# A graph layer's edge pipeline: gathers wait for a nearer sum, two quads go last, additions one step later

## The chip, the cores and the metric

The kernel runs on one core of a Trainium2 chip. TensorE (PE) multiplies matrices, VectorE (DVE) and ScalarE (ACT) work element by element, GpSimd (POOL) issues the indirect DMAs of this kernel, and SyncE (SP) issues most of the other DMAs. The metric is the device time of one execution in microseconds, lower being better.

## The reference, cut to what matters

```python
HIDDEN, NUM_RBF, CUTOFF = 128, 50, 10.0
src, dst = (edge_index[0], edge_index[1])
rbf = jnp.exp(-(distances[:, None] - centers) ** 2 / (2.0 * width * width))
cut = 0.5 * (jnp.cos(jnp.pi * distances / CUTOFF) + 1.0) * (distances <= CUTOFF)
W = (silu(rbf @ fw1 + fb1) @ fw2 + fb2) * cut[:, None]
messages = (h[src] @ pw + pb) * W
agg = jax.ops.segment_sum(messages, dst, num_segments=num_atoms)
L0 = h + (silu(agg @ mw1 + mb1) @ mw2 + mb2)
out = layernorm(x + L0)
```

The call's inputs set the sizes: x has 12,500 rows of 128, and there are 400,000 edges, sorted by destination, with lengths drawn up to 12 and then scaled by 4.688. An edge longer than 10 gives nothing, since its cut is zero. Everything is float32.

## The kernel before

The edges that are no longer than 10 are packed first, in seven chunks, and worked in 139 *quads* (`NL`) of 4 x 128 edges. One step of the main loop does one quad q, and pieces of its neighbours:

- `fetches` issues the indirect DMAs (`fetch`, L1074) that bring the rows `proj[src]` of the quads ahead, four to a quad (`j` 0 to 3), on POOL's queue. The first twelve quads gather x itself and are multiplied by `pw` later (`multiplies`). Eight quads (`SINGLY`) get their j = 0 rows by single-row copies on SP (L1064) and have three gathers. How far ahead POOL runs is set while the program is written: by an estimated clock, by the buffers, and by a wait that `fetch` puts on a gather, for the sum that stood last but `FOLLOW` in the list `last_sum` then.
- `radials` loads the lengths of two quads (tile d) on SP, `basis` makes the radial functions on ACT (L1121, L1122), `first` is the filter's first layer on PE (L1130), `silu` its activation on ACT (L1136); each works on two quads at a time. `second` is the second layer on PE (L1144, L1147), two steps ahead of the quad's message.
- `message` multiplies filter and gathered rows on DVE (L1158). `place` writes the one-hot matrices on DVE (tile hot, L1170) that send each edge to its node within a window of nodes and carry the cutoff factor. `sum_up` multiplies both on PE (L1190), and `add` adds the window to aggT on DVE (L1223).
- `nodes` and `tail` do the node layers as groups of up to four 128-node tiles become complete: `node_first` (L1233, L1234, ACT L1238), `node_second` (L344, L347), the residual and statistics (`node_stats`, L1254, L1259), `deviations` (L1266 to L1270), `scales` (L1277, L1278) and `normalize` (DVE or POOL L1289, ACT L1292), then a store (`node_dma`, L178).

Packing a chunk runs beside the steps: DVE works out where each near edge goes, a scatter on POOL's queue writes the lists (L507, once a chunk), SP loads them back (tile pair), and DVE unpacks them (L852, L853, L882) with transposes on PE (L917). The lists are cleared beforehand by `clear_packed` on SP.

The engines' queues hold what the program's text gives them, in that order; there is no other planner. The order of quads is plain, but for one: `quad_of` takes out the quad `LAST`, which is summed as the very last step, in quarters (`last` in `last_step`), since it belongs to the node tile `END` = 3 alone. Everything after that quad has to end with it: add, node layers, layer norm and store of tile 3.

Of the kernel before, what the change touches and what calls it, by code (L numbers as in the profile page):

```python
# [20 lines left out]
P = 128  # L21
# [8 lines left out]
FOLLOW = 3  # L30
QE = QT * P
# [13 lines left out]
LAST = 26  # L45
# [12 lines left out]
OWN_4 = 66  # L58
DIRECT = 32
# [12 lines left out]
SINGLY = (22, 44, 62, 67, 86, 102, 118, 133)  # L72
# [7 lines left out]
READY = {80: 9, 84: 6, 88: 5, 90: 4}  # L80
# [6 lines left out]
def kernel(  # L87
# [61 lines left out]
    def load_x(t0, n=None):  # L149
        t = x4_sb[loaded[0] % X_BUFS]  # L150
        loaded[0] += 1
        node_dma(t0, t, x, False, n)
        x_sb[t0] = t
# [26 lines left out]
    def quad_of(q):  # L180

        return q if q < LAST or q >= NL else LAST if q == NL - 1 else q + 1

    def steps(k):

        return k if k <= LAST or k >= NL else k - 1
# [637 lines left out]
    def unpack(c):  # L824
# [132 lines left out]
        if QB[c] <= LAST < QB[c + 1]:  # L957
            k = 2 * (LAST - QB[c])
            upto, that = (work.tile([64, 1], F32, name=n, bufs=1)[:np_] for n in ("upto", "that"))
            nc.vector.scalar_tensor_tensor(that, ident[:np_, k:k + 1], -1.0, ident[:np_, k + 1:k + 2],  # L960
                                           op0=OP.mult, op1=OP.subtract)
# [106 lines left out]
    def fetch(q, idx=None, table=None, js=range(QT)):  # L1068
        got = quad_sb[place_of(q) if q >= 0 else 0]
        for j in js:  # L1070
# [6 lines left out]
            if table is None and idx is None and len(last_sum) > FOLLOW:  # L1077
                tc.add_manual_dep(ins.ins, last_sum[-1 - FOLLOW], mybir.DependencyInfo(
# [9 lines left out]
    def radial(o, lengths, eng=nc.sync):  # L1088

        n = math.prod(lengths.shape) // QE  # L1090
        d = work.tile([P, QE], F32, name="d", bufs=3)
        v = lengths.rearrange("(o h) e -> o h e", o=1)
        eng.dma_start(d, v.to_broadcast([64, 2, QE]))
        d_of[o] = d, n
# [3 lines left out]
    def radials(to):  # L1098

        while next_o[0] < min(to, -(-NL // 2)):  # L1100
# [3 lines left out]
            a, b = 2 * quad_of(quads(o)[0]), 2 * quad_of(quads(o)[-1]) + 2  # L1104
            assert b - a == 2 * len(quads(o))
            radial(o, near_d[a:b].rearrange("(h t) e -> h (t e)", t=2))
# [99 lines left out]
    def bases_of(q0, q1):  # L1206

        _, v = nc.values_load_multi_w_load_instructions(
# [3 lines left out]
        for k in range(2 * (q1 - q0)):  # L1212
            bases[q0 + k // 2, k % 2] = v[k]
# [525 lines left out]
```

## Time and profile before

| what | value |
|---|---|
| median of 3 runs | 719.06 us (718.80 to 720.36) |
| profiled execution | 719.15 us |
| its span, first to last instruction | 717.5 us |
| mean granted TensorE clock | 0.917 |
| busy: PE / DVE / ACT / POOL | 590.3 / 561.8 / 397.3 / 536.4 us |
| HBM read / written | 74.59 / 15.79 MB |

The busy times are shares of one span, and no engine reaches it: PE is busy 82%, DVE 78%, POOL 75%, ACT 55%. For POOL the figure leaves out the time between two DMA issues of its own, which the profile books as idle and "issue". In a row of groups stand the line, the engine, the operation, its output and inputs, the count, the busy time with the mean of one in ns, and the idle time before it with what ended most of it. In a timeline row stand the start, the duration, the operation, and in brackets the idle time before it. A row of windows gives the stretch, its length, the busy time of PE, PEld, DVE, ACT and POOL with their instruction counts, the granted PE clock, the DMA engines' busy share and GB/s.

### The profile page before, as it was taken

How to read it: one execution, taken by the hardware profiler on the slowest of the kernel's cores; microseconds unless marked ns; L12 is line 12 of the kernel's file. 1: busy time of each engine (PE TensorE's matmuls, PEld its weight loads, DVE VectorE, ACT ScalarE, POOL GpSimd, SP SyncE). 2: the span in 40 equal slices, each digit the busy share in tenths (PEclk: the TensorE clock that was granted, in tenths of full speed). 3: DMA queues.
4: the chain of work that ended last, by engine and by line, in shares of the span. 5: the costliest groups of instructions: out<-in, count | busy, mean ns of one | idle time of the engine just before them, and what ended most of it. 6: DMA issues, size and time to landing. Idle time of an engine off the chain costs nothing. (4 is left out here: it accounts for less than half of the span.)

```text
span 717.5 us, 13667 instructions
## 1 busy us (share of the span) xinstructions
PE 590.3 (82%) x3524; PEld 465.0 (65%) x3524; DVE 561.8 (78%) x1736; ACT 397.3 (55%) x564; POOL 536.4 (75%) x576
## 2 busy tenths in 40 slices
PE   6887877898889889888588896999987878878884
PEld 5775556776667667576466674787765655656663
DVE  8899799787988999899689895878655455565685
ACT  6557624563645566464348253858744833574474
POOL 7777777777777777777777777777777777777773
PEclk9999687997988999999979997999998999999998
DMA  8995442343334334343333343444433433244342
GB/s 263 348 324 174 149 128 75 87 137 100 98 86 121 97 95 108 97 128 83 94 106 113 98 119 103 137 127 135 136 97 99 148 92 114 84 141 134 96 130 91
DMA packets 53389, 91.35 MB, mean 127 GB/s; under 512 B 13856, under 2 KB 21120, under 8 KB 53306
## 3 DMA queue, kind: packets, MB, share of 16 engines
q1 hardware_dynamic: 34754, 53.20, 22.9%
q0 software_dynamic: 17840, 36.77, 19.8%
q8 instruction: 29, 0.48, 0.3%
q10 hardware_dynamic: 712, 0.46, 0.2%
q14 instruction: 54, 0.44, 0.2%
HBM read 74.59 MB, written 15.79 MB: 126 GB/s over the span
## 5 line engine op out<-in xcount | busy, mean ns | idle before, releaser
L1074 POOL DMA_INDIRECT quad<-proj,srci x421 | 400.6, 952 | 128.4 <-issue 97.6
L1147 PEld LDWEIGHTS bank<-fw_sb,s 128*128 128x128 f32 x1112 | 160.8, 208 | 66.5 <-issue 59.8
L1136 ACT ACTIVATE s<-ph 128x1024 f32<-128x1024 f32 x70 | 71.3, 1018 | 184.4 <-PE ph L1130 184.3
L1147 PE MATMUL bank<-fw_sb,s 128*128 128x128 f32 x1112 | 161.8, 293 | 0.0
L1130 PE MATMUL ph<-rbf,w_sb 102*128 102x512 f32 x278 | 147.1, 655 | 7.5 <-ACT rbf L1122 3.9
L1190 PEld LDWEIGHTS sums<-hot,msg 128*128 128x128 f32 x816 | 112.0, 204 | 54.9 <-issue 27.4
L1170 DVE TENSOR_SCALAR hot<-iota_n,dl,cut 128x80 f32<-128x80 f32 (+4 forms) x408 | 110.1, 344 | 23.6 <-PE sums L1190 21.7
L1190 PE MATMUL sums<-hot,msg 128*128 128x80 f32 (+4 forms) x816 | 113.7, 285 | 15.4 <-DVE msg L1156 7.7
L1144 PE MATMUL bank<-fb_b,ones_b 96*128 96x512 bf16 x139 | 56.1, 404 | 48.8 <-DVE msg L1158 29.8
L1074 POOL DMA_INDIRECT x<-proj,srci x79 | 75.0, 949 | 24.1 <-issue 19.8
L1158 DVE TENSOR_TENSOR msg<-bank,quad 128x512 f32<-128x512 f32 (+1 forms) x82 | 55.7, 679 | 39.4 <-DMA quad<-proj,srci 36.9
L1130 PEld LDWEIGHTS ph<-rbf,w_sb 102*128 102x128 f32 x278 | 52.8, 211 | 48.1 <-issue 38.8
L1223 DVE TENSOR_TENSOR aggT<-aggT,sums 128x80 f32 (+4 forms) x209 | 54.0, 258 | 32.5 <-PE bank L1234 11.7
L1121 ACT ACTIVATE rbf<-d,rbf_bias,rbf_scale 102x512 f32<-102x512 f32 x70 | 56.2, 803 | 14.8 <-DMA d<-near_d 14.7
L1074 POOL DMA_INDIRECT quad<-in_x_dram,srci x48 | 47.6, 992 | 14.8 <-issue 11.9
L347 PEld LDWEIGHTS bank<-pw_sb,xT 128*128 128x128 f32 (+1 forms) x292 | 42.0, 207 | 8.0 <-issue 4.0
L1122 ACT ACT_TABLE_LOAD x35 | 44.9, 1283 | 0.6
L1136 ACT ACT_TABLE_LOAD x35 | 44.9, 1283 | 0.6
L1122 ACT ACTIVATE rbf<-rbf 102x512 f32<-102x512 f32 x70 | 44.1, 630 | 1.5
L1190 PE MATMUL sums<-quad,quad 128*128 128x104 f32 (+3 forms) x296 | 40.9, 281 | 3.9 <-DVE quad L1158 3.9
L1170 DVE TENSOR_SCALAR quad<-iota_n,dl,cut 128x104 f32<-128x104 f32 (+3 forms) x148 | 40.5, 348 | 3.9 <-issue 2.8
L1158 DVE TENSOR_TENSOR quad<-bank,quad 128x512 f32<-128x512 f32 (+2 forms) x40 | 25.2, 632 | 23.4 <-DMA quad<-proj,srci 16.1
(282 smaller groups left out, 803.0 us busy)
## 6 DMA issues: line engine op xcount, KB each, us to landing
d<-near_d SPq DMA_DIRECT2D x70, 256.0 KB
dl<-proj SPq DMA_DIRECT2D x1024, 0.5 KB
x<-in_x_dram SPq DMA_DIRECT2D x45, 256.0 KB
quad<-proj,srci POOLq DMA_INDIRECT x421
proj<-hp SPq DMA_DIRECT2D x24, 256.0 KB
out_dram<-x SPq DMA_DIRECT2D x21, 256.0 KB
r_d<-in_edge_weight_dram SPq DMA_DIRECT2D x5, 256.0 KB
r_dst<-in_dst_dram SPq DMA_DIRECT2D x5, 256.0 KB
```

Source lines behind the costliest of these rows:

```text
L347: nc.tensor.matmul(to[:m, k, :], lT[:, k * P:k * P + m], w, start=False, stop=(k == a + c - 1))
L1074: ins = nc.gpsimd.indirect_dma_start(out=got[:, j, :], out_offset=None, in_=proj if table is None else table, in_offset=bass.IndirectOffse ...
L1121: nc.scalar.activation(rbf[:u], d[:u], AF.Square, bias=rbf_bias[:u], scale=rbf_scale[:u])
L1122: nc.scalar.activation(rbf[:u], rbf[:u], AF.Exp, scale=-1.0 / (2.0 * width * width))
L1130: nc.tensor.matmul(ph[:, h, :], w1_sb[:2 * KR, h, :], rbf[:2 * KR], start=True, stop=True)
L1136: nc.scalar.activation(s[:, :n], ph[:, :n], AF.Silu)
L1144: nc.tensor.matmul(pu, ones_b[:, :P], bias_b["fb2"].rearrange("k j f -> k (j f)"), start=True, stop=False)
L1147: nc.tensor.matmul(pu[:, j * H:(j + 1) * H], s[:, j * P:(j + 1) * P], fw2_sb, start=False, stop=(j == QT - 1))
L1158: nc.vector.tensor_mul(msg[:, a:b, :], pu_of[q].rearrange("p (j f) -> p j f", j=QT)[:, a:b, :], got_of[q][:, a:b, :])
L1170: nc.vector.tensor_scalar(hot[:, j, :wide(q)], iota_n[:, :wide(q)], dl[:, at[0], at[1]], cut[:, at[0], at[1]], op0=OP.is_equal, op1=OP.mult)
L1190: ins = nc.tensor.matmul(pa[:, k * W:k * W + wide(q)], msg[:, j, :], hot[:, j, :wide(q)], start=(j % n == 0), stop=(j % n == n - 1))
L1223: nc.vector.tensor_add(to, to, pa[:, k * W:k * W + wide(q)])
```

## The change

Five things are changed.

1. A gather that is written once twenty sums stand in the program (`NEARER`) waits for the sum one further back than the newest (`NEAR` = 1), where it was three further back.
2. The additions of a step come after the next step's message on DVE, up to 15 steps from the end.
3. `first` and `silu` are issued in every even step, once, where it was in steps 0 and 1 of every four; from step 32 on (`SHIFT`) they run one pair of quads further ahead, and `basis` moves with them.
4. Two quads, 25 and 26, are left for the last two steps, where it was 26 alone. The other node groups move a step earlier (`READY`, `tail`), and `last_step` is written anew: tile 3 has its residual added on PE by a product with the identity, its statistics by bn_stats and bn_aggr, and one scaling. Its rows are loaded at step 70 and doubled on ACT at step 74.
5. The clears of `packed` are four DMAs in place of fourteen, d is loaded in two pieces where its quads aren't neighbours, and the SINGLY quads 44 and 67 become 43 and 66.

The diff, cut to its core:

```diff
+NEARER = 20
+NEAR = 1
...
-LAST = 26
+LAST = 25
+N_LAST = 2
...
+SHIFT = 32
...
-SINGLY = (22, 44, 62, 67, 86, 102, 118, 133)
+SINGLY = (22, 43, 62, 66, 86, 102, 118, 133)
...
-READY = {80: 9, 84: 6, 88: 5, 90: 4}
+READY = {80: 9, 84: 7, 88: 6, 90: 5, 93: 4, 95: 3}
...
+        late = q - (NL - N_LAST)
+        return q if q < LAST or q >= NL else LAST + late if late >= 0 else q + N_LAST
...
-            if table is None and idx is None and len(last_sum) > FOLLOW:
-                tc.add_manual_dep(ins.ins, last_sum[-1 - FOLLOW], mybir.DependencyInfo(
+            back = FOLLOW if len(last_sum) < NEARER else NEAR
+            if table is None and idx is None and len(last_sum) > back:
+                tc.add_manual_dep(ins.ins, last_sum[-1 - back], mybir.DependencyInfo(
...
-        for i in range(LISTS if k == 0 else 3):
-            v = packed[i, a:b].rearrange("(p w) -> p w", p=P)
-            for w0 in range(0, (b - a) // P, 376):
-                n = min(376, (b - a) // P - w0)
-                eng.dma_start(v[:, w0:w0 + n], zero_i[:, :n])
+        m = LISTS if k == 0 else 3
+        v = packed[:m, a:b].rearrange("s (p w) -> p s w", p=P)
+        for w0 in range(0, (b - a) // P, 376):
+            n = min(376, (b - a) // P - w0)
+            eng.dma_start(v[:, :, w0:w0 + n], zero_i[:, None, :n].to_broadcast([P, m, n]))
...
-    def last_step(q, msg):
+    def last_step(q):
         assert not ready and not deep and not singles
-        bases_of(q, NL - 1)
-        roots = deviations([84, 88, 90], st_of[3][:, 4:])
-        nc.scalar.activation(warm, half_pi, AF.Silu)
+        place(q)
+        node_stats(93, st_of[1][:, 9:])
+        msg = message(q)
+        node_second(95)
         tc.mark_branch_hint_location("rest", some, [
             mybir.EngineType.DVE, mybir.EngineType.PE, mybir.EngineType.Pool])
-        keep_busy(5)
+        keep_busy(2)
         sum_up(q, msg)
-        assert done_to(2 * q + 2) >= 95 * P
-        node_first(93)
+        node_stats(95, st_of[1][:, 11:])
+        nc.scalar.activation(warm, half_pi, AF.Sqrt)
         def last(j):
             sum_up(NL - 1, message(NL - 1, (j, j + 1)), (j,))
         last(0)
+        roots = deviations([84, 88, 90, 93, 95], st_of[1])
+        nc.scalar.activation(warm, half_pi, AF.Silu)
+        add(q)
+        keep_busy(2)
+        last(1)
         scales(*roots)
-        add(q)
-        node_first(95)
-        last(1)
-        normalize(*ready.pop(0))
-        for n in (2, 3):
-            normalize(*ready.pop(0), on=range(n), v=nc.gpsimd)
-        node_second(93)
+        of = {r[0]: r for r in ready}
+        ready.clear()
+        normalize(*of[93], on=range(2))
+        normalize(*of[90])
+        normalize(*of[84], on=range(4), v=nc.gpsimd)
+        keep_busy(2)
         last(2)
-        node_second(95)
+        keep_busy(1)
+        pz, py = bank(), bank()
+        nc.tensor.matmul(pz[:, :P], bias_b["mb1"][:, 0, :], ones_b[:, :P], start=True, stop=False)
+        nc.tensor.matmul(py[:, :H], ones_b[:, :P], bias_b["mb2"][:, 0, :], start=True, stop=False)
+        nc.tensor.matmul(py[:, :H], ident, end_sb[:, 0, :], start=False, stop=False)
         last(3)
-        node_stats(93, st_of[1], lambda: add(NL - 1))
-        node_first(END)
-        node_stats(95, st_of[1][:, 2:])
-        node_second(END)
-        node_stats(END, st_of[1][:, 5:])
-        scales(*deviations([93, 95, END], st_of[1]))
-        normalize(*ready.pop(0), on=(0, 1), v=nc.gpsimd)
-        normalize(*ready.pop(0), on=(0, 1), eng=nc.scalar)
-        normalize(*ready.pop(0), on=(0,))
-        assert not ready
+        add(NL - 1)
+        normalize(*of[95], on=range(3))
+        normalize(*of[88], on=range(2), v=nc.gpsimd)
+        nc.tensor.matmul(pz[:, :P], mw1_sb, aggT[:, END * P:(END + 1) * P], start=False, stop=True)
+        zs = work.tile([P, QE], F32, name="zs", tag="hp", bufs=3)[:, :P]
+        nc.scalar.activation(zs, pz[:, :P], AF.Silu)
+        nc.tensor.matmul(py[:, :H], zs, mw2_sb, start=False, stop=True)
+        st, mv = keep.tile([P, 6], F32, name="st_end"), keep.tile([P, 2], F32, name="mv_end")
+        nc.vector.bn_stats(st, py[:, :H])
+        nc.vector.bn_aggr(mv, st)
+        dev = keep.tile([P, 2], F32, name="dev_end")
+        nc.scalar.activation(dev[:, 0:1], mv[:, 1:2], AF.Sqrt, bias=eps)
+        nc.vector.reciprocal(dev[:, 1:2], dev[:, 0:1])
+        nc.vector.tensor_scalar(end_sb[:, 0, :], py[:, :H], mv[:, 0:1], dev[:, 1:2],
+                                op0=OP.subtract, op1=OP.mult)
+        free.extend((pz, py))
+        node_dma(END, end_sb, out, True)
...
         msg = message(q)
+        while to_add:
+            add(to_add.pop(0))
...
+        if q == NODES:
+            node_dma(END, end_sb, x, False)
+        if q == NODES + 4:
+            nc.scalar.activation(end_sb, end_sb, AF.Copy, scale=2.0)
         if loads_later and q >= 8:
             nc.sync.dma_start(*loads_later.pop(0))
-        radials(q // 2 + 5)
+        radials(q // 2 + (5 if q < SHIFT else 6 + q % 4 // 2))
         one_by_one()
         multiplies(q + 1 + EARLY_X)
         if q + 2 < NL:
             second(q + 2)
-        if q % 4 < 2 and 2 * octs(q) < NL:
-            first(octs(q))
-            silu(octs(q))
-        if q % 4 == 3:
+        while q % 2 == 0 and 2 * ahead[0] < min(NL, q + (6 if q < SHIFT else 8)):
+            first(ahead[0])
+            silu(ahead[0])
+            ahead[0] += 1
+        if q % 4 == (3 if q < SHIFT else 1):
...
-            add(k)
+            if q < NL - 15:
+                to_add.append(k)
+            else:
+                add(k)
         tail(q)
```

How the rows of the engines' queues move, at three places. The lines of the kernel after are some ten higher: L1141 for L1130, L1155 and L1158 for L1144 and L1147, L1169 for L1158, L1181 for L1170, L1201 for L1190 and L1225 for L1223.

PE at steps 16 to 18, before (ph is the first layer's output, bank the second layer's, sums the window sums):

```order
260 L1130 MATMUL ph<-rbf,w_sb 128x512 x2
261 L1190 MATMUL sums<-hot_1071,msg_1076 128x56 x4
262 L1144 LDWEIGHTS ones_b
263 L1144 MATMUL bank_168<-fb_b,ones_b 128x512
264 L1147 MATMUL bank_168<-fw_sb,s 128x128 x4
265 L1130 MATMUL ph<-rbf,w_sb 128x512 x2
266 L1190 MATMUL sums<-hot_1190,msg_1218 128x56 x4
267 L1144 LDWEIGHTS ones_b
268 L1144 MATMUL bank_170<-fb_b,ones_b 128x512
269 L1147 MATMUL bank_170<-fw_sb,s 128x128 x4
270 L1190 MATMUL sums<-hot_1071,msg_1076 128x56 x4
```

and after:

```order
260 L1141 MATMUL ph<-rbf,w_sb 128x512 x2
261 L1201 MATMUL sums<-hot_1065,msg_1070 128x56 x4
262 L1155 LDWEIGHTS ones_b
263 L1155 MATMUL bank_168<-fb_b,ones_b 128x512
264 L1158 MATMUL bank_168<-fw_sb,s 128x128 x4
265 L1201 MATMUL sums<-hot_1184,msg_1208 128x56 x4
266 L1155 LDWEIGHTS ones_b
267 L1155 MATMUL bank_170<-fb_b,ones_b 128x512
268 L1158 MATMUL bank_170<-fw_sb,s 128x128 x4
269 L1141 MATMUL ph<-rbf,w_sb 128x512 x2
270 L1201 MATMUL sums<-hot_1065,msg_1070 128x56 x4
```

The first layer that stood ahead of the sum of step 17 now stands ahead of that of step 18; step 17 has none.

DVE at steps 15 and 16, before (msg is the message, hot the one-hot matrices, the ISA rows set an addition's address, nodes and r_d belong to packing):

```order
391 L1158 TENSOR_TENSOR msg_1218<-bank_170,x_90 128x512
392 L1200 TENSOR_LOAD base_i x2
393 L1170 TENSOR_SCALAR hot_1071<-iota_n,dl,cut 128x56 x4
394 L1223 ISA
395 L1223 TENSOR_TENSOR aggT<-aggT,sums 128x56
396 L1223 ISA
397 L1223 TENSOR_TENSOR aggT<-aggT,sums 128x56
398 L532 SCALAR_TENSOR_TENSOR nodes<-bank_167,nodes 128x512
399 L522 COPY_PREDICATED nodes<-bank_167,nodes 128x448
400 L522 COPY_PREDICATED r_d<-bank_167,r_d 128x448
401 L1158 TENSOR_TENSOR msg_1076<-bank_169,x_91 128x512
```

and after:

```order
392 L1169 TENSOR_TENSOR msg_1208<-bank_170,x_90 128x512
393 L1211 TENSOR_LOAD base_i x2
394 L1181 TENSOR_SCALAR hot_1065<-iota_n,dl,cut 128x56 x4
395 L537 SCALAR_TENSOR_TENSOR nodes<-bank_167,nodes 128x512
396 L527 COPY_PREDICATED nodes<-bank_167,nodes 128x448
397 L527 COPY_PREDICATED r_d<-bank_167,r_d 128x448
398 L1169 TENSOR_TENSOR msg_1070<-bank_169,x_91 128x512
399 L1225 ISA
400 L1225 TENSOR_TENSOR aggT<-aggT,sums 128x56
401 L1225 ISA
402 L1225 TENSOR_TENSOR aggT<-aggT,sums 128x56
403 L1181 TENSOR_SCALAR hot_1184<-iota_n,dl,cut 128x56 x4
```

The two additions left the place behind the one-hot matrices of step 15 and stand behind the message of step 16.

DVE at the very end, before (end is tile 3, x_90 the group at tile 95, st the statistics):

```order
1573 L1259 BN_STATS st<-x_90 128x6 x2
1574 L1259 BN_STATS st<-x_90 84x6
1575 L1254 SCALAR_TENSOR_TENSOR end<-end,bank_170 128x128
1576 L1259 BN_STATS st<-end 128x6
1577 L1266 TENSOR_TENSOR dif<-st 128x6
1578 L1267 TENSOR_TENSOR both_m<-st 128x12
1579 L1268 SCALAR_TENSOR_TENSOR dif<-dif 128x6
1580 L1269 TENSOR_TENSOR v<-both_m,dif 128x6
1581 L1277 RECIPROCAL rs<-dev 128x6
1582 L1278 SCALAR_TENSOR_TENSOR by<-both_m,rs 128x6
1583 L1289 TENSOR_SCALAR x_90<-x_90,rs,by 128x128 x2
1584 L1289 TENSOR_SCALAR end<-end,rs,by 128x128
```

and after:

```order
1547 L1169 TENSOR_TENSOR quad_79<-bank_168,quad_86 128x128 x2
1548 L1225 ISA
1549 L1225 TENSOR_TENSOR aggT<-aggT,sums 128x80
1550 L1291 TENSOR_SCALAR x_90<-x_90,rs,by 128x128 x2
1551 L1291 TENSOR_SCALAR x_90<-x_90,rs,by 84x128
1552 L1428 BN_STATS st_end<-bank_170 128x6
1553 L1429 BN_AGGR mv_end<-st_end 128x2
1554 L1432 RECIPROCAL dev_end<-dev_end 128x1
1555 L1433 TENSOR_SCALAR end<-bank_170,mv_end,dev_end 128x128
```

Group 95 is scaled ahead of the last tile's statistics, the addition of the residual and five small operations are gone, and the scaling reads PSUM.

More of the change, by code (lines that the diff above doesn't have):

```diff
@@ L1204, in base_of @@
             bases[q, k] = v[0]
[L1206 to L1213 removed]
     def added(q):
[L1217 removed]
+        return max((q - 2) // 2 * 2 if q < NL - 14 else q - 1 if q < NL - 5 else q, 0)
     def add(q, ks=(0, 1)):
@@ L1559 @@
     clock[0] += 1.3
-    def octs(q):
-        return q // 4 * 2 + 2 + q % 4
-    some, counted = None, []
+    some, counted, to_add, ahead = None, [], [], [2]
     for q in range(NL - 2):
```

66 lines of the change are left out of this document (34 added, 32 removed).

## The prediction, made before the changed kernel ran

> **What bounds the kernel now.** I read the page's costliest groups first, then the waits of POOL and DVE, the busy time by windows, and the timelines of the places where the change can act. The first row says where the time goes: 421 of the indirect gathers, which POOL issues itself.
>
> ```profile
> L1074 POOL DMA_INDIRECT quad<-proj,srci x421 | 400.6, 952 | 128.4 <-issue 97.6
> L1074 POOL DMA_INDIRECT x<-proj,srci x79 | 75.0, 949 | 24.1 <-issue 19.8
> L1074 POOL DMA_INDIRECT quad<-in_x_dram,srci x48 | 47.6, 992 | 14.8 <-issue 11.9
> ```
>
> Each row has the busy time, the mean length in ns, and the idle time ahead. 421 + 79 + 48 = 548 gathers, and their busy and idle time sum to 400.6 + 75.0 + 47.6 + 128.4 + 24.1 + 14.8 = 690.5 us of the 717.5 us span. POOL's longest list of waits is this:
>
> ```profile
> POOL quad L1074 <- issue: 109.5, 359, 0.3
> ```
>
> The third number is the longest wait: no gather counted there waited more than 0.3 us. So POOL waits for nobody; it spends its own 1.26 us for each gather (690.5 / 548), from the first to the last. The windows show the same belt in the middle and near the end (PE, PEld, DVE, ACT, POOL busy us in 20 us, each with its instructions):
>
> ```profile
> 440.00:460.00 20.00, 19.32 (x110) 14.41 (x110) 13.53 (x53) 13.30 (x21) 15.18 (x16) 0.88 0.40 117
> 600.00:620.00 20.00, 15.71 (x90) 11.44 (x89) 10.57 (x35) 9.02 (x10) 15.12 (x17) 0.91 0.35 104
> ```
>
> At 440 to 460 us PE is nearly full (19.32 of 20), yet POOL's 16 or 17 instructions go on at the same rate, since gathers run ahead of their use. At 600 to 620 us neither PE nor DVE is full: they wait for gathers.
>
> ```profile
> DVE msg L1158 <- DMA quad<-proj,srci: 36.9, 17, 4.0
> DVE hot L1170 <- PE sums L1190: 21.7, 14, 3.8
> ```
>
> The first row is those waits. The second lies in the first half of the kernel, where the gathers are tens of us ahead. The end is therefore the POOL belt plus the work after its last gather. Speeding up PE or DVE in between buys nothing by itself; a pause on POOL is never made up.
>
> **The change part by part.** The times below belong to the profiled execution: 719.15 us, with a span of 717.5; the median of the three runs is 719.06, so the sum needs no further shift than 0.09.
>
> *The tighter wait.* Gathers issued once 20 sums are in the program wait for the sum one quad back instead of three back. A waiting gather holds the whole POOL queue: every later gather, the packing scatters (L507), and through these DVE's packing. I compared the start of each gather with the end of the sum it would now wait for, counting gathers from the start (4 to a quad, 3 for the eight quads that get one row otherwise). With the old distance no gather comes closer to its sum than 4.6 us; with the new one two regions have negative slack. The first is early: the first gather of quad 34 would wait for the sum of quad 18 (counted from 0), and a gather of quad 41 for the sum of quad 28.
>
> ```profile
> 180.98 0.94 POOL L1074 DMA_INDIRECT x<-proj,srci  x1 [0.30 <-issue]
> 181.03 1.00 PE L1190 MATMUL sums<-hot,msg 128*128 128x56 f32 x8
> 221.22 0.95 POOL L1074 DMA_INDIRECT quad<-proj,srci  x1 [0.30 <-issue]
> 223.58 1.02 PE L1190 MATMUL sums<-hot,msg 128*128 128x80 f32 x8
> ```
>
> The sums end at 182.03 and 224.60. With 0.25 us for POOL to go on after a wait (my estimate, from the 0.30 us that POOL idles between any two gathers) the shifts are 182.03 + 0.25 - 180.98 = 1.30 us and 224.60 + 0.25 - 221.22 = 3.63 us; they are not added, the later one contains the earlier. So with before's sums the early price is 3.6 us. It falls to nothing if the sum of quad 28 comes 3.6 us sooner. The second region is late: the first gather of quad 86 to be tied (443.74) to the sum of quad 80, and one of quad 89 (460.05) to that of quad 84.
>
> ```profile
> 437.31 0.46 PE L917 MATMUL bank<-ident,f_src 54*128 54x54 f32 x2 [4.53 <-DVE f_src L882]
> 439.07 1.92 PE L1147 MATMUL bank<-fw_sb,s 128*128 128x128 f32 x8
> 440.78 3.62 PE L1130 MATMUL ph<-rbf,w_sb 102*128 102x512 f32 x4
> 444.19 1.34 PE L1190 MATMUL sums<-hot,msg 128*128 128x80 f32 x8
> 443.74 0.94 POOL L1074 DMA_INDIRECT quad<-proj,srci  x1 [0.31 <-issue]
> 459.07 1.05 PE L1147 MATMUL bank<-fw_sb,s 128*128 128x128 f32 x8
> 461.68 1.02 PE L1190 MATMUL sums<-hot,msg 128*128 128x80 f32 x8
> 460.05 0.94 POOL L1074 DMA_INDIRECT quad<-proj,srci  x1 [0.30 <-issue]
> ```
>
> 444.19 + 1.34 + 0.25 - 443.74 = 2.0 us, and 461.68 + 1.02 + 0.25 - 460.05 = 2.9 us in all. After about 480 us the gathers lead so little that their sums are long done, and the wait costs nothing.
>
> *First layer every even step.* Before, two steps of four carry L1130 and two carry none; now each even step carries one. Counted over steps, PE has issued the same number of L1130 groups by the sums of steps 0, 2 and 3 of each four, and one fewer by step 1 (the pair further ahead from step 32 on is one extra, paid once). The sums of quads 18, 24, 28, 80 and 84 are such steps, so the order alone brings them nothing. What can move the early ones is the clock:
>
> ```profile
> 163.00:166.00 3.00, 1.12 (x10) 0.97 (x10) 2.96 (x8) 2.72 (x5) 2.10 (x3) 0.83 0.37 120
> 166.00:169.00 3.00, 2.60 (x12) 2.51 (x12) 2.93 (x10) 0.96 (x1) 2.38 (x3) 0.50 0.39 130
> 172.21 3.37 PE L1130 MATMUL ph<-rbf,w_sb 102*128 102x512 f32 x4
> 177.36 1.88 PE L1130 MATMUL ph<-rbf,w_sb 102*128 102x512 f32 x4
> 176.46 1.01 DVE L1170 TENSOR_SCALAR hot<-iota_n,dl,cut 128x56 f32<-128x56 f32 x4 [3.82 <-PE sums L1190]
> ```
>
> In the light steps 14 and 15 PE is busy 1.12 of 3 us, then its granted clock is 0.50, the L1130 group of step 16 takes 3.37 instead of 1.88 us, and DVE waits 3.82 us. Now step 14 has a group of its own (1.88 us) just in that gap. If this keeps the clock up, the wait at 176 and its like later shrink; those 3.8 us are about what quad 28 needs, and more than the 1.3 of quad 18. I take the early price as 0, near the row of the removed wait, with 3.6 as its other end. The Trainium skill, TensorE: Matmul & The Clock Gate, What's actually happening in Part 1, says that the array drops to half clock after an idle window of about 3.4 us. The early spells do not fit it strictly, for PE was still busy 1.12 of 3 us before the drop, so it doesn't promise that the extra group ends them.
>
> The late place is different. Its 4.53 us of PE idleness hangs on POOL itself:
>
> ```profile
> 427.19 0.99 POOL L507 DMA_INDIRECT packed<-line,at_i  x1 [0.30 <-DVE x L1254]
> 434.75 0.46 DVE L852 TENSOR_TENSOR two<-pair 54x256 int32<-54x256 int32 x1 [3.31 <-DMA pair<-packed]
> ```
>
> The last packing scatter leaves POOL at 427.19; DVE waits 3.31 us for what it wrote; f_src and the message of quad 80 follow, and PE resumes. A faster PE or DVE before that point only waits longer. Step 80 itself has the same work in the same order in both kernels. So I take the late price whole, 2.9 us, with 2.0 as its lower end where quad 84 gains 0.9 us meanwhile. By the same section of the Trainium skill a 4.53 us gap gives the half clock again, which the 3.62 us row agrees with; by it the late price stays as it is.
>
> *Additions a step later.* DVE does L1223 after the next message, outside the last 15 steps. The instructions are the same; a message no longer stands behind an addition that waits. Where PE is full or gathers are late this moves the end by nothing: 0, from -0.5 (quad 84 earlier) to 0.5 (an addition now behind a message that waits up to 4.0 us for its gather).
>
> *SP and small things.* Fourteen clears become four DMAs of the same bytes, first-layer distances go in two pieces to a load, two quads with a separately copied row change their number (43, 66), and the final tile's rows are loaded at step 70 and doubled by ACT, which is busy under 15 of 20 us in the windows above. POOL's order of gathers stays, and SP has time for all this: 0.
>
> *The end.* Two quads are left for the last steps instead of one, so the other groups are through a step earlier, and the last tile gets a chain of its own. Before, after the last gather:
>
> ```profile
> 703.62 0.94 POOL L1074 DMA_INDIRECT quad<-proj,srci  x1 [0.30 <-issue]
> 708.19 0.35 PE L1190 MATMUL sums<-quad,quad 128*128 128x80 f32 x2
> 708.58 0.24 DVE L1223 TENSOR_TENSOR aggT<-aggT,sums 128x80 f32 x1 [0.80 <-PE sums L1190]
> 709.45 0.28 ACT L1238 ACTIVATE zs<-bank 128x128 f32<-128x128 f32 x1 [0.74 <-PE bank L344]
> 709.75 1.28 ACT L1270 ACT_TABLE_LOAD   x1
> 709.78 0.49 PE L347 MATMUL bank<-mw_sb,zs 128*128 128x128 f32 x2 [0.37 <-ACT zs L1238]
> 710.31 0.29 DVE L1254 SCALAR_TENSOR_TENSOR end<-end,bank 128x128 f32<-128x128 f32 x1
> 711.05 0.16 DVE L1267 TENSOR_TENSOR both_m<-st 128x12 f32<-128x12 f32 x1
> 711.56 0.30 ACT L1270 ACTIVATE dev<-v,eps 128x6 f32<-128x6 f32 x1 [0.53 <-DVE v L1269]
> 711.90 0.19 DVE L1277 RECIPROCAL rs<-dev 128x6 f32<-128x6 f32 x1 [0.37 <-ACT dev L1270]
> 712.33 0.60 DVE L1289 TENSOR_SCALAR x<-x,rs,by 128x128 f32<-128x128 f32 x2
> 712.84 0.34 DVE L1289 TENSOR_SCALAR end<-end,rs,by 128x128 f32<-128x128 f32 x1
> 713.96 0.40 SPq L178 DMA_DIRECT2D out_dram<-end  x1
> ```
>
> Up to the second layer's matmul I leave the times, since DVE and PE have a backlog there in both. Then, now: matmul done at 710.27; the residual is already in its PSUM sum, so bn_stats follows at once (0.3, as the tile-wide addition whose place it takes) and bn_aggr (0.2) replaces the four small operations; both end by 710.8, before the Sqrt table load does (709.75 + 1.28 = 711.03). ACT's root 0.30 to 711.35, reciprocal 0.2 to 711.6, one scaling of the tile 0.34 to about 712.0, and the store issues near 712.05 instead of 713.96: 1.9 us less. bn_aggr isn't in the trace; I price it between the 0.16 us of the small operation at 711.05 and the 0.29 of the tile-wide one at 710.31, and the table load covers either. Ends: 1.2 where DVE's three scalings of tile 95, now ahead of bn_stats, are late by 0.7; 2.8 where the shorter queue of earlier groups also brings the last sum 0.9 us forward (DVE waited 0.8 us for that sum, which stood behind other work on PE).
>
> **Sum:** 719.15 + 2.9 (late) + 0 (early) + 0 - 1.9 = 720.15, and 0.09 less at the median's level: 720.1 us.
>
> **The rivals.**
> 1. *Both stalls stay, slower.* If the half clock of the light steps persists, the sum of quad 28 is where it is now, and POOL's belt takes 3.6 early and 2.9 late, for the late sum hangs on the belt and moves with it. 719.06 + 3.6 + 2.9 - 1.9 = 723.7 us. It decides from a quad-28 sum that is less than 3.6 us sooner against its gather. For it: the order brings these sums nothing by itself, and 140 to 220 us has little slack. Against: DVE's 21.7 us of waits for sums, of which a good part should go.
> 2. *No stall, faster.* If PE has its full clock at step 80, that step's second layer, first layer and sum are shorter by 1.92 - 1.05, 3.62 - 1.88 and 1.34 - 1.02, together 2.9 us; the sum ends near 442.6, ahead of 443.74. Quad 84 gains as much. Then 719.06 - 1.9 = 717.2 us. For it: only 1 to 3 us are missing. Against: the 4.53 us gap.
> 3. *The wait does nothing* (the program's other waits cover it): also 717.2 us, by another road. Against: the four negative slacks above.
> 4. *The end brings nothing*, because the last gathers' landing or the other stores hold it: 719.06 + 2.9 = 722.0 us.
>
> **How the numbers follow.** Forecast 0.42, rival 1 0.17, rival 2 0.27, rival 3 0.05, rival 4 0.09. The forecast's own range is 719.06 + 2.0 - 2.8 = 718.3 to 719.06 + 2.9 - 1.2 + 0.5 = 721.3. A measurement tells 0.2% from no change, 1.44 us: 717.62 to 720.50. Of the forecast 0.02 falls below this, 0.28 in it, 0.12 above; rivals 2 and 3 give 0.25 below and 0.07 in it (tail 1.2); rival 1 is above, and so is rival 4 but for a small part. Faster 0.27, same 0.35, slower 0.38. The range goes from 716.8 (no stall, tail of 2.3) to 722.8 (early price of 2.7): it leaves out the far ends of rivals 1 and 2, less than 2 in 10.
>
> **What would show it.** POOL's waits for PE sums at L1190 should rise, with one of about 2 us at the first gather after 443 us and one of about 1 us some 16 us on; the windows there should hold one or two POOL instructions fewer. Between 180 and 225 us there should be none. The last gather should start near 703.6 + 2.9 = 706.5, and the span from it to the last store's issue should be near 8.4 us instead of 10.3. DVE's waits for sums in L1170 should fall by several us. I am wrong if POOL's stream ends within 1 us of 703.6, if the stalls lie elsewhere than in these two regions, or if that last stretch is as long as before.

## The result, and the profile after

The change makes the kernel slower: 736.9 us (median of 6 runs, 734.37 to 740.73) against 719.65 (6 runs), a ratio of 1.024, 95% interval 1.0204 to 1.0276. The prediction was 720.1 us with 722.8 as its upper end; the loss is some 17 us where about one was expected. The profiled execution took 739.09 us, with a span of 737.5.

POOL's row of gathers and its waits are those that answer to the first rows of before:

```profile
L1080 POOL DMA_INDIRECT quad<-proj,srci x421 | 399.5, 949 | 144.6 <-issue 101.2
POOL quad L1080 <- issue: 113.9, 373, 0.5
POOL quad L1080 <- PE sums L1201: 12.4, 10, 4.2
POOL quad L1080 <- PE bank L975: 6.6, 2, 4.5
POOL x L1080 <- PE sums L1201: 2.9, 2, 1.5
```

A gather takes as long as before (949 ns), but POOL now waits, up to 4.5 us at a time, for sums (the row of L975 is a small matmul that ended last by the profile, beside the sum). The pauses in POOL's timeline, start, duration, and in brackets the idle time ahead, of which 0.30 is POOL's own:

```profile
182.21 0.94 POOL L1080 DMA_INDIRECT x<-proj,srci  x1 [1.48 <-PE sums L1201]
207.22 0.94 POOL L1080 DMA_INDIRECT x<-proj,srci  x1 [1.46 <-PE sums L1201]
243.03 0.94 POOL L1080 DMA_INDIRECT quad<-proj,srci  x1 [2.04 <-PE bank L975]
390.18 0.94 POOL L1080 DMA_INDIRECT quad<-proj,srci  x1 [3.04 <-PE sums L1201]
436.19 0.99 POOL L512 DMA_INDIRECT packed<-line,at_i  x1 [2.04 <-DVE line L504]
455.38 1.00 POOL L1080 DMA_INDIRECT quad<-proj,srci  x1 [3.00 <-PE sums L1201]
464.65 0.94 POOL L1080 DMA_INDIRECT quad<-proj,srci  x1 [0.78 <-PE bank L922]
472.61 0.94 POOL L1080 DMA_INDIRECT quad<-proj,srci  x1 [4.52 <-PE bank L975]
480.25 0.94 POOL L1080 DMA_INDIRECT quad<-proj,srci  x1 [4.20 <-PE sums L1201]
722.98 0.95 POOL L1080 DMA_INDIRECT quad<-proj,srci  x1 [0.30 <-issue]
```

Less 0.30 each, these nine sum to 19.9 us, and two small ones at 409 and 423 add 0.5. The last gather starts at 722.98 instead of 703.62, 19.4 us later. So the belt of gathers is still what the span is made of, and its pauses are the loss. Both regions had been named, the early one (180 to 245 us) at a price of 0 and the late one (445 to 480 us) at 2.9 us; the pause at 390, the scatter at 436 that waits for DVE, and the size of the late ones had not.

What is new at 375 to 392 us is on DVE and ACT. One of DVE's waits, before (L338) and after (L343), then its places in after, on ACT, DVE and PE, and a window of PE's clock:

```profile
DVE mb_f L338 <- ACT part L334: 1.2, 1, 1.2
DVE mb_f L343 <- ACT part L339: 7.4, 2, 4.9
377.71 0.81 ACT L1132 ACTIVATE rbf<-d,rbf_bias,rbf_scale 102x512 f32<-102x512 f32 x1
381.20 0.63 ACT L1133 ACTIVATE rbf<-rbf 102x512 f32<-102x512 f32 x1
381.73 0.28 ACT L339 CAST part<-mb_f 96x128 bf16<-96x128 f32 x1
382.05 0.29 DVE L343 TENSOR_TENSOR mb_f<-mb_f,part 96x128 f32<-96x128 f32 x1 [2.51 <-ACT part L339]
383.25 0.59 PE L1155 MATMUL bank<-fb_b,ones_b 96*128 96x512 bf16 x1 [4.48 <-DVE quad L1169]
385.34 3.62 PE L1141 MATMUL ph<-rbf,w_sb 102*128 102x512 f32 x4
388.76 1.15 PE L1201 MATMUL sums<-quad,quad 128*128 128x112 f32 x8
389.00 1.02 ACT L1147 ACTIVATE s<-ph 128x1024 f32<-128x1024 f32 x1 [5.03 <-PE ph L1141]
389.92 0.29 ACT L339 CAST part<-mb_f 96x128 bf16<-96x128 f32 x1
390.23 0.29 DVE L343 TENSOR_TENSOR mb_f<-mb_f,part 96x128 f32<-96x128 f32 x1 [4.91 <-ACT part L339]
385.00:388.00 3.00, 3.00 (x7) 1.44 (x7) 0.33 (x2) 0.00 (x0) 1.83 (x2) 0.50 0.26 65
```

In steps 62 to 67 the node biases are split into bf16 pieces: ACT casts (L339), DVE subtracts (L343). The cast of step 65 (381.73) stood behind that step's basis (from 377.71 on), DVE waited 2.51 us, its next message was late, PE idled 4.48 us and then ran the first layer at half clock (0.50 granted from 385 to 388 us; 3.62 us, where the same operation takes 1.88). The sum behind it ended at 389.91 us, and the gather that waited for it started at 390.18. The cast of step 66 stood behind the activation (L1147) of that very first layer; DVE waited 4.91 us more. Before, the whole kernel had 1.2 us of such waits. It is not DVE's only longer wait: those for sums at the additions (L1225) rose from 9.4 to 17.3 us.

The end of after, from the last sum:

```profile
730.11 0.35 PE L1201 MATMUL sums<-quad,quad 128*128 128x80 f32 x2
732.50 0.18 DVE L1429 BATCH_NORM_AGGREGATE mv_end<-st_end 128x2 f32<-128x6 f32 x1
732.90 0.29 ACT L1431 ACTIVATE dev_end<-mv_end,eps 128x1 f32<-128x1 f32 x1
733.43 0.41 DVE L1433 TENSOR_SCALAR end<-bank,mv_end,dev_end 128x128 f32<-128x128 f32 x1
733.87 0.33 SPq L182 DMA_DIRECT2D out_dram<-end  x1
```

From the end of the last sum to the store's issue are 733.87 - 730.46 = 3.4 us; before it was 713.96 - 708.54 = 5.4. But the last sum ended 7.5 us behind the last gather's start, where it was 4.9.

### The profile page after: what moved, and what is told of

The parts are those of the page before. It is cut to its first block, busy times and chain, and to the rows that moved or that the text cites. A ratio compares the mean times of both kernels' runs of the same rounds, so it can differ in the third digit from the quotient of the medians.

```text
span 737.5 us, 13640 instructions
## 1 busy us (share of the span) xinstructions
PE 603.1 (82%) x3528; PEld 473.6 (64%) x3528; DVE 562.7 (76%) x1735; ACT 394.6 (54%) x563; POOL 535.3 (73%) x575
## 5 line engine op out<-in xcount | busy, mean ns | idle before, releaser
L1158 PEld LDWEIGHTS bank<-fw_sb,s 128*128 128x128 f32 x1112 | 166.1, 214 | 60.9 <-issue 51.9
L1147 ACT ACTIVATE s<-ph 128x1024 f32<-128x1024 f32 x70 | 71.2, 1017 | 204.7 <-PE ph L1141 204.3
L1158 PE MATMUL bank<-fw_sb,s 128*128 128x128 f32 x1112 | 166.1, 299 | 0.0
L1141 PE MATMUL ph<-rbf,w_sb 102*128 102x512 f32 x278 | 146.2, 652 | 7.7 <-ACT rbf L1133 4.1
L1201 PEld LDWEIGHTS sums<-hot,msg 128*128 128x128 f32 x816 | 110.0, 204 | 47.0 <-DVE aggT L1225 19.7
L1181 DVE TENSOR_SCALAR hot<-iota_n,dl,cut 128x80 f32<-128x80 f32 (+4 forms) x408 | 109.9, 347 | 27.3 <-PE sums L1201 24.4
L1201 PE MATMUL sums<-hot,msg 128*128 128x80 f32 (+4 forms) x816 | 113.7, 286 | 17.2 <-DVE aggT L1225 12.9
L1155 PE MATMUL bank<-fb_b,ones_b 96*128 96x512 bf16 x139 | 57.9, 417 | 40.8 <-DVE msg L1169 16.2
L1169 DVE TENSOR_TENSOR msg<-bank,quad 128x512 f32<-128x512 f32 (+1 forms) x82 | 55.4, 676 | 44.1 <-DMA quad<-proj,srci 31.7
L1141 PEld LDWEIGHTS ph<-rbf,w_sb 102*128 102x128 f32 x278 | 53.4, 214 | 48.6 <-issue 39.1
L1225 DVE TENSOR_TENSOR aggT<-aggT,sums 128x80 f32 (+4 forms) x209 | 53.4, 256 | 24.5 <-PE sums L1201 17.3
L1236 PE MATMUL bank<-aggT,mw_sb 128*128 128x512 f32 (+3 forms) x52 | 31.7, 695 | 21.6 <-DVE aggT L1225 21.6
L1201 PEld LDWEIGHTS sums<-quad,quad 128*128 128x128 f32 x296 | 39.5, 200 | 11.0 <-issue 8.5
L352 PE MATMUL bank<-pw_sb,xT 128*128 128x128 f32 (+1 forms) x292 | 42.7, 294 | 0.6 <-ACT xT L1016 0.6
L1181 DVE TENSOR_SCALAR quad<-iota_n,dl,cut 128x80 f32<-128x80 f32 (+3 forms) x148 | 40.2, 341 | 2.6 <-issue 1.9
```

What stands on the lines that cost most here:

```text
L352: nc.tensor.matmul(to[:m, k, :], lT[:, k * P:k * P + m], w, start=False, stop=(k == a + c - 1))
L1141: nc.tensor.matmul(ph[:, h, :], w1_sb[:2 * KR, h, :], rbf[:2 * KR], start=True, stop=True)
L1147: nc.scalar.activation(s[:, :n], ph[:, :n], AF.Silu)
L1155: nc.tensor.matmul(pu, ones_b[:, :P], bias_b["fb2"].rearrange("k j f -> k (j f)"), start=True, stop=False)
L1158: nc.tensor.matmul(pu[:, j * H:(j + 1) * H], s[:, j * P:(j + 1) * P], fw2_sb, start=False, stop=(j == QT - 1))
L1169: nc.vector.tensor_mul(msg[:, a:b, :], pu_of[q].rearrange("p (j f) -> p j f", j=QT)[:, a:b, :], got_of[q][:, a:b, :])
```

## The experiments

Two theories stood at the start. Theory 1: the near wait costs what the sum says, 6.5 us, and the rest is *slip*, sums made late by another part of the change and handed on to POOL by the wait. Theory 2: the wait feeds itself, as a late gather delays packing and later sums. (The expectation of e1 calls something else Theory 2: late sums that reach the end without the near wait.) Medians are set against runs of the kernel before on the same chip (719.4 us beside e1 to e4, 720.2 beside e5 to e8, 719.8 beside e12 to e14). The edits are to the changed kernel, unless another is named.

**The near wait alone** (kernel before, e2):

```diff
-            if table is None and idx is None and len(last_sum) > FOLLOW:
-                tc.add_manual_dep(ins.ins, last_sum[-1 - FOLLOW], mybir.DependencyInfo(
+            back = FOLLOW if len(last_sum) < NEARER else NEAR
+            if table is None and idx is None and len(last_sum) > back:
+                tc.add_manual_dep(ins.ins, last_sum[-1 - back], mybir.DependencyInfo(
```

> The kernel before with the near wait alone. By the sum in the prediction, with before's own sums: 3.6 us early and 2.9 late, 719.6 + 6.5 = 726 us, POOL pausing near 181, 205, 221, 444 and 460 us and nowhere else. Theory 1 (slip by the other edits): this, 724 to 728. Theory 2 (the wait feeds itself: a late gather delays packing and this the sums that the next gathers wait for): 732 us or more, with pauses that repeat between 440 and 480 us.

Measured: 728.64 us (ratio 1.0128, 1.0108 to 1.0148), 9.2 us more than the kernel before, with 7.8 as the lower end; the sum said 6.5. The profiled execution, the fastest of the four, took 725.16, 6.0 more than that of before. POOL's longer pauses in it:

```profile
181.46 0.94 POOL L1076 DMA_INDIRECT x<-proj,srci  x1 [1.12 <-PE sums L1193]
207.83 0.94 POOL L1076 DMA_INDIRECT x<-proj,srci  x1 [2.81 <-PE sums L1193]
309.51 0.94 POOL L1076 DMA_INDIRECT quad<-proj,srci  x1 [0.95 <-PE bank L971]
449.39 0.94 POOL L1076 DMA_INDIRECT quad<-proj,srci  x1 [1.47 <-PE sums L1193]
466.55 0.94 POOL L1076 DMA_INDIRECT quad<-proj,srci  x1 [1.15 <-PE sums L1193]
```

Less 0.30 each: 0.8 + 2.5 early (with 0.35 at 224.8, not shown, 3.7; the sum said 3.6), 0.65 at 309 that it did not have, 1.2 + 0.85, together 2.0, late (it said 2.9). In this execution the places and the total hold, the pauses don't repeat, and Theory 2 falls for the kernel before. The median is 3.5 us worse than this one execution and lies above the 724 to 728 of Theory 1; where those went no trace shows.

The late half alone (`NEARER` = 60, kernel before, e13):

> The same kernel as e10 (before with the near wait only from the 60th sum on), on a chip where the kernel before takes about 720 us. By the late term 2.9 us and two pauses near 444 and 460: 722.5 to 723.5 us. If the early half is what later sums pay for, 720 to 721; if the late region alone feeds itself, 726 or more.

Measured: 721.28 us, ratio 1.0015 (0.9998 to 1.0033), less than expected. The trace is that of the slowest of ten executions (723.92 us). It has the two pauses expected, 2.5 us less 0.30 each, and the wait is as cheap there as the sum said, or cheaper:

```profile
77.95 0.94 POOL L1076 DMA_INDIRECT x<-proj,srci  x1 [3.18 <-DVE srci L924]
447.72 0.94 POOL L1076 DMA_INDIRECT quad<-proj,srci  x1 [1.93 <-PE sums L1193]
464.89 0.94 POOL L1076 DMA_INDIRECT quad<-proj,srci  x1 [1.15 <-PE sums L1193]
```

The first row is a pause of 2.9 us for packing on DVE, long before the near wait holds here. The traces of before and of e1 have none there, and that of e5 has one of 2.0; so single executions differ by some 3 us where no edit reaches. By the medians the late half costs 1.5 us of the 9.2, and the early half would then cost 7.7 (e2 and e13 ran on two chips), where its pauses in e2's trace come to 3.7.

**All but the near wait** (e1)**:**

```diff
-NEAR = 1
+NEAR = 3
```

> The changed kernel, its gathers waiting for the sum three back again. Theory 1 (slip): the other edits make the sums between 375 and 480 us later by some 8 to 10 us against the gathers, and the near wait passes this on to POOL; with the far wait POOL has 5 to 7 us of room there, so its stalls fall from 21 us to 0 to 5, and the time is 718 to 724 us. Theory 2 (the late sums reach the end by themselves, through the packing scatter or the messages): still above 728 us. The end, as the changed trace has it, is 0.6 us longer than before, so below 719 would be against both.

Measured: 727.0 us, ratio 1.0102 (1.0083 to 1.012). Ten of the 17 us are gone, but the time lies between the two theories, and both were too simple: POOL pauses without the near wait as well, at the scatter that waits for DVE, and once for long (and 1.0 us at 148 to 150). For the long pause the profile names no releaser, and its cause isn't shown.

```profile
429.56 0.99 POOL L512 DMA_INDIRECT packed<-line,at_i  x1 [1.60 <-DVE line L504]
498.64 0.94 POOL L1080 DMA_INDIRECT quad<-proj,srci  x1 [3.97 <-issue]
```

**The old order of first layer, activation and basis, with the near wait** (e4)**:**

```diff
-        while q % 2 == 0 and 2 * ahead[0] < min(NL, q + (6 if q < SHIFT else 8)):
-            first(ahead[0])
-            silu(ahead[0])
-            ahead[0] += 1
-        if q % 4 == (3 if q < SHIFT else 1):
+        if q % 4 < 2 and 2 * (q // 4 * 2 + 2 + q % 4) < NL:
+            first(q // 4 * 2 + 2 + q % 4)
+            silu(q // 4 * 2 + 2 + q % 4)
+        if q % 4 == 3:
```

(and `radials(q // 2 + 5)` again.)

> The changed kernel with the old order of the first layer, its activation and the basis (two steps in four, nothing further ahead). If the new order is what makes the sums late (ACT's queue in steps 62 to 67, basis at another step), the near wait has its 6.5 us and no more: 719.6 + 6.5 + 0.6 = 727 us. If the later additions or the wait itself make the sums late, it stays at 733 us or more.

Measured: 723.88 us, ratio 1.0064 (1.0042 to 1.0085), 13 us less than the changed kernel and below the expectation. In the trace, of the fastest of four executions, an early pause of 0.4 and late ones of 0.8 and 0.9 us are left:

```profile
445.04 1.03 POOL L1080 DMA_INDIRECT quad<-proj,srci  x1 [1.07 <-PE sums L1201]
462.20 0.94 POOL L1080 DMA_INDIRECT quad<-proj,srci  x1 [1.16 <-PE sums L1201]
```

So of the 17 us, 13 go with the new order and 10 with the near wait: the two overlap, and the order is the larger. It has two parts, and `SHIFT = NL` keeps the first alone (every even step, never further ahead, basis in step 3 of four), with the near wait (e5) and with the far one (e8):

> The changed kernel with the first layer in every even step but never a pair further ahead, and the basis where it was (step 3 of four). If running a pair further ahead with the basis in step 1 is what makes the sums late, this comes near the kernel with the old order: 722 to 727 us. If the every-even-step order does it, 731 us or more.

> The changed kernel with the far wait, every even step, never further ahead. If the sums' lateness comes from running further ahead, 717 to 720 us, as with the old order; if from the every-even-step order, about the 727 us of the far wait alone.

Measured: 726.33 us (ratio 1.0081, 1.0052 to 1.011) and 721.42 us (1.0023, 0.9999 to 1.0048), the second above the 717 to 720 expected of it. Every even step costs about 2 us, at the edge of the intervals; running a pair further ahead, with the basis in step 1, costs 5.6 us with the far wait (727.0) and 10.6 with the near one (736.9).

What is left when wait and order are both as before, with the later additions (e6) and without (e7, whose edit is shown):

```diff
-            if q < NL - 15:
-                to_add.append(k)
-            else:
-                add(k)
+            add(k)
```

> The changed kernel with the far wait and the old order of first layer and basis: what is left is the later additions, the new end and the small things. No pause on POOL beyond before's 0.6, and by the traces of the other runs (last instruction 12.9 to 14.5 us after the last gather, 13.9 before) 717.5 to 719.5 us; if later additions cost something by themselves, above 721.

> The same with the additions back in their own step: the new end and the small things alone. By the prediction's 1.9 us for the end, 717.5; if an equal backlog takes it back, as it did in the changed kernel's trace, 719.0 to 720.0.

Measured: 719.61 us (0.9991, 0.9976 to 1.0005), 0.1 above the expectation, and 718.52 us (0.9972, 0.9959 to 0.9986), between the two cases of its own. The new end and the small things alone are a gain, 2.0 us by the ratio; the later additions give about one of them back, at the edge of the intervals. What they do move is a wait of DVE for a small matmul of the final count of packed edges (L1471), here without the later additions and with them:

```profile
DVE miss L1471 <- PE bank L1470: 0.3, 1, 0.3
DVE miss L1471 <- PE bank L1470: 5.5, 1, 5.5
```

The count now starts on DVE ahead of the additions, its matmul stands behind a step's work on PE, and the next message stands behind that. The wait is 5.5 to 5.9 us in after and in every run above and below with later additions (e1, e3 to e6, e8, e12), and 0.3 in those without (before, e2, e7, e13, e14). Whether it is the one microsecond isn't shown.

**The bias pieces out of ACT's queue's way.** The six pieces are issued ahead of the step's first layer, activation and basis, instead of at the step's end, with the near wait (e3) and with the far one (e12):

```diff
         while to_add:
             add(to_add.pop(0))
+        if NODES - 8 <= q < NODES - 2:
+            part_of(*(("mb1", mb1_f) if q < NODES - 5 else ("mb2", mb2_f)), (q - NODES + 8) % 3)
         nodes(q)
```

> The changed kernel, the splitting of the node biases (six small pieces of ACT and DVE work in steps 62 to 67) put ahead of the step's first layer, activation and basis instead of behind the sum. If ACT's queue there (the basis with its table loads, and an activation that waits for PE, ahead of a piece that DVE waits for) makes the sums late, DVE's waits for L339 of 7.4 us go, POOL's pause of 3.0 us near 390 goes, and the time falls by 5 to 10 us, to 727 to 732. If those waits are hidden, within 1.5 us of the changed kernel (736.9).

> The same kernel as e9 (far wait, bias pieces ahead of first layer, activation and basis), on a chip where the kernel before takes about 720 us. If those pieces behind ACT's basis and activations are all that running further ahead costs (727.0 against 721.4 for the far wait), 720 to 723 us; if other short ACT work that DVE waits for costs as much, 724 to 727.

Measured: 730.75 us (1.0158, 1.0109 to 1.0207) and 719.09 us (0.9988, 0.9969 to 1.0007). DVE's waits for the pieces in the second (in the first one of 3.2 us is left):

```profile
DVE mb_f L343 <- ACT part L339: 0.5, 1, 0.5
```

With the far wait this one move takes 7.9 us off, and all that the new order cost is gone: there, the clash of the pieces with ACT's longer work was the whole of it. With the new order and the pieces early, the near wait still costs 11.7 us (730.75 against 719.09); with the old order it is 4.3 (723.88 against 719.61). In the profile of e3 POOL pauses 6.2 us early (at 185, 210 and 246 us) and 5.0 between 452 and 474. The longest of the late ones, followed back:

```profile
463.74 1.63 ACT L1294 ACTIVATE x<-x,by,rs 128x128 f32<-128x128 f32 x4
465.28 0.58 ACT L1240 ACTIVATE zs<-bank 128x512 f32<-128x512 f32 x1
465.90 0.38 PE L1155 MATMUL bank<-fb_b,ones_b 96*128 96x512 bf16 x1 [2.59 <-ACT zs L1240]
467.01 1.02 PE L1201 MATMUL sums<-quad,quad 128*128 128x80 f32 x8
468.30 0.94 POOL L1080 DMA_INDIRECT quad<-proj,srci  x1 [2.71 <-PE bank L975]
```

The activation of a node layer (L1240) stands behind the scaling of finished tiles (L1294) on ACT, PE waits 2.59 us for it, the sum behind ends at 468.03 us, and POOL goes on 0.27 us later. This wait of 2.59 us is in all five kernels that run a pair further ahead (after, e1, e3, e12, e14); in the others the second layer's matmul waits for this activation for 1.2 us at most. So the new order has a second clash of the same kind: the far wait hides it (e12 has it and no pause behind it), the near one passes it on. No run takes it out, so its price isn't measured, and the early pauses stay open. The order of the steps up to 32 is the same in after, e3 and e5, and the two pauses near 183 and 208 us came to 2.3, 4.5 and 2.9 us in their traces.

By the medians the near wait costs 9.2 us on the kernel before, 4.3 with the old order, 4.9 with every even step alone (e5 against e8), 9.9 in the changed kernel and 11.7 with the pieces early. Its price is no constant, and why it is 9.2 on the kernel before and 4.3 with the old order and the rest of the change isn't shown.

**The additions in their own step, with the new order and the far wait** (e14)**:**

> The same kernel as e11 (far wait, new order of the first layer, additions in their own step), on a chip where the kernel before takes about 720 us. If the later additions cost the same 1.1 us as with the old order, 725.5 to 726.5 us; if they are what lets the new order lose, 721 to 723; if they soften it, above 728.

Measured: 725.17 us (1.0068, 1.0042 to 1.0094), just below the expectation and 1.8 less than with the later additions (e1, on another chip, with an interval that overlaps); they may add a little to either order. The bias pieces cost as much here, and the scatter waits longest, which shows the slip's other road to POOL:

```profile
DVE mb_f L343 <- ACT part L339: 7.9, 2, 5.3
431.52 0.99 POOL L512 DMA_INDIRECT packed<-line,at_i  x1 [4.61 <-DVE line L504]
```

**Runs that tell nothing on this.** Seven runs came at a time when the kernel before itself took 1003 to 1014 us on their chips; no number there is set beside the others. There were three such chips, and the one of e17 and e18 is that of e12 to e14, on which the kernel before had taken 719.77 us about eleven minutes earlier. The kernels of e12 to e14 are those of e9 to e11. The other four were for a version better than both, the far wait with pieces early and additions in their own step, and the new end again; they are e15 to e18.

> The changed kernel with the far wait and the bias pieces put ahead of the step's first layer, activation and basis. If those pieces behind ACT's basis and activations are all that running further ahead costs (727.0 against 721.4 for the far wait), 720 to 723 us; if other short ACT work that DVE waits for (the cosine of the packing, the node layers) costs as much, 724 to 727.

> The kernel before with the near wait only from the 60th sum on. By the prediction's late term, 2.9 us and two pauses near 444 and 460 us: 722.5 to 723.5. If the early half of the wait is what later sums pay for, 720 to 721; if the late region alone feeds itself, 726 or more.

> The changed kernel with the far wait and the additions in their own step again. With the old order of the first layer the later additions cost 1.1 us. If they add to the new order in the same way, 725.5 to 726.5 us. If they are what lets the new order lose (DVE no longer held up by an addition, but at the next ACT piece), 721 to 723; if they soften it, above 728.

> The changed kernel with the far wait, the bias pieces early and the additions in their own step: new end, small things, and the new order of the first layer without its clash. If the order without the clash costs nothing, as the kernel with the new end alone: 718 to 719 us, ratio 0.997 to 0.998. If later additions were needed to make the order harmless, above 720.

> The same kernel as e7 (new end and small things alone) beside it: 718.5 us, ratio 0.996 to 0.999 again.

> The same kernel as e15, on a chip where the kernel before takes about 720 us: 718 to 719 us, ratio 0.997 to 0.998, if the new order of the first layer costs nothing without its clash; above 720 if later additions were needed to make it harmless.

> The same kernel as e7 and e16 beside it, on a chip where the kernel before takes about 720 us: 718.5 us, ratio 0.996 to 0.999 again.

Measured there: 992.03, 971.43 and 989.58 us (before 1003.24); 1010.25 and 1021.54 (before 1013.21); 1005.59 and 1012.12 (before 1014.05). Whether the pieces moved early would improve on the new end alone stays open. The best version with a number is e7, at 718.52 us.

## Why the prediction was wrong, point by point

- *What bounds the kernel.* Right. POOL's belt sets the end, a pause there is not made up, and the last gather's 19.4 us account for the profile's loss.
- *The near wait.* The mechanism and the two regions were right, and in the one traced execution of e2 the sizes for before's sums: 3.6 and 2.9 us expected, 3.7 and 2.0 measured. By its median the wait alone costs 9.2 us; the other 3 aren't accounted for. What failed is that the slack of the wait was treated as fixed, while the rest of the change made the sums later. That a late sum at 440 to 480 us is then paid in full is argued from the pauses there, not shown gather by gather.
- *The early price taken as 0.* Wrong; rival 1 was right here. The light spell moved with the extra first layer and did not go. Two windows of PE's clock and DVE's wait in after:

```profile
166.00:169.00 3.00, 1.51 (x7) 1.42 (x7) 2.93 (x9) 2.94 (x5) 2.33 (x3) 0.68 0.22 56
169.00:172.00 3.00, 3.00 (x15) 2.91 (x15) 2.64 (x8) 1.85 (x2) 2.38 (x3) 0.50 0.52 148
176.37 0.97 DVE L1181 TENSOR_SCALAR hot<-iota_n,dl,cut 128x56 f32<-128x56 f32 x4 [2.65 <-PE sums L1201]
```

  PE was busy 1.51 us in three, the clock fell to 0.50, and DVE waited 2.65 instead of 3.82 us there (over the kernel its waits for sums in this line rose from 21.7 to 24.4 us, where a fall was forecast); the sum of quad 18 ended within 0.1 us of where it was, and the early pauses came to 4.1 us. The doubt in the prediction, that the drop comes without the idle window that TensorE: Matmul & The Clock Gate of the Trainium skill names in What's actually happening of Part 1, held: again no gap of 3.4 us stands ahead of it.
- *First layer every even step: "the order alone brings them nothing".* This is the step that failed most: put at nothing, the order cost 7.4 us with the far wait (727.0 against 719.61, e1 and e6) and 13 with the near one (736.9 against 723.88, e4). Only PE's queue was counted. The move also changes what stands ahead of short work on ACT, of which the prediction says only, and for another edit, that it is busy under 15 of 20 us. That share was no evidence: a cast of 0.3 us behind a basis, and another behind an activation that waits for PE, held up DVE, through DVE the messages, through them PE and its clock, and so the sums. Moving six small pieces took away 7.9 us with the far wait, all of the order's cost there, and 6.2 with the near one.
- *The late price, 2.9 us.* The rows were right and their premise, "step 80 itself has the same work in the same order", too; but the sums came to it late, the scatter waited for DVE (1.7 us), and from 455 to 481 us the pauses came to 11.3 us.
- *Additions: 0, from -0.5 to 0.5.* Probably too small: 1.1 and 1.8 us slower by the medians, with intervals that overlap. The wait of 5.5 to 5.9 us that they bring at the count was overlooked; what it costs is not shown.
- *The end, 1.9 us.* The chain from the last sum was 2.0 us shorter, as worked out; the time that the new end and the small things bring alone is 2.0 us by the ratio. In the changed kernel the last sum came 2.6 us later behind the last gather, and the whole stretch to the store was 10.9 us, not 8.4.
- *The rivals.* None had a wait between ACT and DVE. Rival 1's 723.7 us has the right sign and is 13 us short.

## What to carry to other kernels

When an edit moves an instruction, list what stands behind it on every engine that it touches, above all the short operations that another engine waits for: ACT was busy 54% of the span here, and a 0.3 us cast stood behind what came ahead of it all the same. A wait that is tightened should be priced with the sums that the rest of the change will leave: where its slack is small, lateness from elsewhere becomes its price. Time the parts alone and together: here one gained 2 us, one cost 9 by itself, and the same wait cost from 4.3 to 11.7 us beside different neighbours.

## What the runs showed that was not expected

In the seven runs set apart above all kernels took 1.4 times as long. The kernel of e11 there, its group of POOL's gathers and a wait of PE's weight loads:

```profile
L1080 POOL DMA_INDIRECT quad<-proj,srci x421 | 400.5, 951 | 289.8 <-issue 155.5
PEld bank L1158 <- issue: 144.9, 81, 18.0
```

A gather takes 951 ns as ever, but engines stand up to 18 us for nothing that the profile names, and the mean TensorE clock is 0.815 against 0.928 for the same kernel (e14). The chip recorded for e17 and e18 had run the kernel before in 719.77 us shortly before, so the slowness isn't a fixed property of a chip. Its cause isn't known.
